# Token numbers in place of token rows in the slots of a grouped mixture of experts, and gathers in place of plain loads

## The chip, the core and the metric

The kernel runs on one core of a Trainium2 chip. The metric is the device time of one execution in microseconds. An execution taken with the hardware profiler gives the views that are read here; its times are in microseconds from the start of the span, unless said otherwise. The engines are TensorE (PE, with its weight loads PEld), VectorE (DVE), ScalarE (ACT), GpSimd (POOL) and SyncE (SP, which here only issues transfers).

## The reference, cut to what matters

The program is a chain of four blocks on x, 1250 tokens of 512 numbers, each with a residual: a message-passing layer over 40,000 edges, a grouped mixture of experts, a two-layer graph attention network, and an expert-choice mixture. The change concerns the second:

```python
z = layernorm(x, ln_g, ln_b)
gw = topk_gate(x @ wg_group, 2, G)                  # G = 4 groups
for g in range(G):
    iw = topk_gate(z @ wg_inner[g], 2, E)           # E = 8 experts in a group
    moe = sum(iw[:, e] * (relu(z @ W1[g, e] + b1[g, e]) @ W2[g, e] + b2[g, e]) for e in range(E))
    out += gw[:, g] * layernorm(z + moe, gln_g[g], gln_b[g])
```

As only two of four groups count for a token, and two of eight experts in each, a token needs four of the 32 experts: 5000 pairs of token and expert.

## The kernel before, in words

Everything is float32. 1250 tokens are ten chunks of 125 (`P`), a chunk's tokens on the partitions. The stages follow one another in one program, and a scheduler that knows the tiles places the waits; each engine runs its instructions in the order in which they were built.

**The edge stage** (0 to some 740 us) sorts the edges and runs 45 beats over them. In each beat a function `side(s)` does something besides: it stores two blocks of 128 rows of zeros (256 KB each) to `zs_d`, 88 in all, on SP's queue (L1996), until all of `zs_d` holds zeros; and it makes small products for the attention later. The sums of the edges go to the DRAM tile `sums_d`.

**The experts' slots.** In DRAM `zs_d` has 32 times `SL` = 208 rows, one stretch of slots for each expert, and behind these the rows of tiles of 128 for what does not fit in an expert's 208. Before the change a slot holds a token's row of 512 numbers, then the expert's output for it, in the same place.

**`grouped_moe`** does this in order:

1. For each of five blocks (`blk`) of two chunks: load the sums (`acc`, SP, L77), transpose them on TensorE (`transpose`, L95), project, add to x, normalise. VectorE and then POOL (L1008, one addition for each chunk) make the rows `z`. ScalarE and TensorE make the logits (`nT` L998, `lg` L1003), `top2` picks groups and experts.
2. Still in the block: a product with a triangular matrix on TensorE (L1027) counts how many earlier tokens chose the same expert, and so gives each pair its place in the slots; VectorE makes the four slots of each token (`slots`, `p4i`, L1040). Then POOL issues eight indirect DMAs (two chunks, four pairs, L1043), each of which scatters 125 rows of `z`, 2 KB each, to `zs_d`. A pair beyond 208 has a slot out of bounds and is dropped.
3. In blocks 1 and 2 the call `adjacency` makes a part of the graph's adjacency for the attention: SP loads `adj`, TensorE transposes it (L95), ScalarE does two operations for each piece (`none` L829, `adjt` L830), POOL adds them (L831) and issues the stores to `adjT_d` (L77). Parts 0 and 1 are done here, parts 2 to 4 in the loop over experts (e = 1, 4, 7). After block 1 `load` issues the weights of experts 0 to 5 on SP (L879, L881).
4. After the blocks: the counts (L1056), where experts have more than 208 pairs (`more`, L1058, `te`, L1077), the place of every pair in `pair_slot` and, with the slots that fit sent out of bounds, in `over_slot`. Scores become weights, x takes its share (L1120).
5. The loop over 32 experts: `rows(e)` loads the expert's 208 rows as two halves of 104 (`zr`, SP, L1132), issued two experts ahead; TensorE transposes them (`pz`, L95) and does the first layer (`ph`, L1150), ScalarE the relu (`hT`, L1152), TensorE the second layer (`po`, L1159), VectorE adds the rows (`y`, L1161), and ScalarE's queue stores y to the same slots (L1162).
6. Under `tc.If(some > 0)` the tiles beyond: 40 scatters with `over_slot`, then a loop over the tiles that are used. With these inputs no expert has more than 208 pairs and this part is not run.
7. For each chunk POOL gathers the four outputs of each token by `pair_slot` (`ya`, L1215), VectorE and ScalarE normalise and weight them, and the attention stage begins.

What sets the order around the change: POOL runs scatters, additions of z, additions of adjt and the issue of adjT_d's stores in one line. SP runs the loads of weights, sums, adjacency and rows in one line. A DMA that must wait holds what is behind it on its queue.

The step that the change is about, and the load that reads it:

```python
st = nc.gpsimd.indirect_dma_start(
    out=zs_d, out_offset=bass.IndirectOffsetOnAxis(ap=p4i[:, i, j:j + 1], axis=0),
    in_=z[:, blk * BC + i, :], in_offset=None, bounds_check=GX * SL - 1, oob_is_err=False)
...
def rows(e):
    zr = sp.tile([HS, 2, D], F32, name="zr", bufs=4)
    nc.sync.dma_start(zr, zs_d[e * SL:(e + 1) * SL, :].rearrange("(j p) d -> p j d", p=HS))
```

Of the kernel before, what the change touches and what calls it, by code (L numbers as in the profile page):

```python
# [52 lines left out]
MOE_NT = max(4 * -(-(N - MOE_SL) // MOE_TS), (4 * N - 5 * (MOE_SL + 1 - MOE_TS)) // MOE_TS)  # L53
MOE_ROWS = 32 * MOE_SL + MOE_NT * MOE_TS
LN_EPS = 1e-5
# [779 lines left out]

def grouped_moe(k, x, sums_d, nb_d, adjT_d, finish, zs_d, W_out0, W_out1, ln_g, ln_b, wg_group, wg_inner,
                W1, b1, W2, b2, gln_g, gln_b):


# [7 lines left out]
    HC = H // 128  # L847
    SL, TS, NT = MOE_SL, MOE_TS, MOE_NT
    HS = SL // 2
# [4 lines left out]
    with ExitStack() as es:  # L854
        mp = es.enter_context(tc.tile_pool(name="moe", bufs=1, reuse_waits="tile"))
        pair_slot = mp.tile([P, NC, 4], I32, name="pair_slot")
        over_slot = mp.tile([P, NC, 4], I32, name="over_slot")
        iw = [[mp.tile([P, NC], F32, name=f"iw{a}{b}") for b in range(2)] for a in range(2)]
# [12 lines left out]
        teri = mp.tile([1, NT + 1], I32, name="teri")  # L871
        b1T = mp.tile([128, GX * HC], F32, name="b1T")
        sw = ExitStack()
# [10 lines left out]
        with ExitStack() as s1:  # L884
# [86 lines left out]
            for blk in range(NB):  # L971
# [69 lines left out]
                for i in range(BC):  # L1041
                    for j in range(4):
                        st = nc.gpsimd.indirect_dma_start(  # L1043
                            out=zs_d, out_offset=bass.IndirectOffsetOnAxis(ap=p4i[:, i, j:j + 1], axis=0),
                            in_=z[:, blk * BC + i, :], in_offset=None, bounds_check=GX * SL - 1,
                            oob_is_err=False)
# [76 lines left out]
        with ExitStack() as s2:  # L1123
# [43 lines left out]
            for e in range(GX):  # L1167
# [5 lines left out]
                if e + 2 < GX:  # L1173
                    zr.append(rows(e + 2))
                zT = expert(zT, w1, w2, b1T[:, e * HC:(e + 1) * HC], 2, HS,
                            lambda: turned(zr.pop(0), 2, HS) if zr else None,
                            zs_d[e * SL:(e + 1) * SL, :])

            some = nc.values_load(teri[0:1, NT:NT + 1], min_val=0, max_val=NT,
                                  skip_runtime_bounds_check_because="a count of tiles")  # L1180
            with tc.If(some > 0):
                for c in range(NC):
                    for j in range(4):
                        st = nc.gpsimd.indirect_dma_start(
                            out=zs_d, out_offset=bass.IndirectOffsetOnAxis(ap=over_slot[:, c, j:j + 1],
                                                                          axis=0),
                            in_=z[:, c, :], in_offset=None, bounds_check=MOE_ROWS - 1, oob_is_err=False)
                        tc.declare_no_dep(st.ins, group="beyond", reason="slots of different pairs")
                        tc.add_to_no_dep_group("beyond", st.ins)
                for i in range(NT):  # L1190
# [7 lines left out]
                    nc.sync.dma_start(b, b1f[bass.ds(e, 1)].rearrange("o (k p) -> p (o k)", p=128))  # L1198
                    r0 = GX * SL + i * TS
                    z1 = sp.tile([TS, 1, D], F32, name="z1")  # L1200
# [744 lines left out]
def kernel(  # L1945
# [13 lines left out]
    xup_d = dram.tile([N, SW], F32, name="xup_d")  # L1959
    sums_d = dram.tile([CARRY + 256, SUMS], F32, name="sums_d")  # L1960
    nb_d = dram.tile([NC, P, N], BF16, name="nb_d")
# [3 lines left out]
    r_d = dram.tile([NC * 8, P], F32, name="r_d")  # L1965
    zs_d = dram.tile([MOE_ROWS, D], F32, name="zs_d")
    n_d = dram.tile([N, D], F32, name="n_d")
# [5 lines left out]
    with ExitStack() as turned:  # L1973
        with tc.tile_pool(name="xres", bufs=1, reuse_waits="tile") as xp:
# [13 lines left out]
            with tc.tile_pool(name="keep", bufs=1, reuse_waits="tile") as keep:  # L1988
# [14 lines left out]
            def finish():  # L2003
# [5 lines left out]

            grouped_moe(k, x, sums_d, nb_d, adjT_d, finish, zs_d, W_out0, W_out1, ln_g, ln_b, wg_group, wg_inner, fW1, fb1, fW2, fb2,  # L2010
                        gln_g, gln_b)
# [32 lines left out]
```

## Time and profile before

| | |
|---|---|
| time, median of ten runs | 2285.82 us (2278.57 to 2298.63) |
| profiled execution, its own time | 2285.86 us |
| its span | 2284.1 us, granted TensorE clock 0.915 |
| HBM read, written | 326.25 MB, 133.33 MB |
| `zs_d<-zero` stores | 88 of 256 KB, started between 112 and 684 us |
| `zs_d<-z` scatters | 40, median 1192 ns, started between 828.0 and 925.0 us |
| `zr<-zs_d` loads | 32 of 416 KB, started between 932.9 and 1151.0 us |
| `ya` gathers | 40, median 1211 ns, started between 1185.9 and 1260.2 us |

In the profile a group of instructions is named by line, engine, operation and the tiles out<-in, with the partitions and the elements of each. In a timeline a row gives the start, the busy time, and in brackets how long the engine was idle before and what released it. Neighbouring instructions of one kind are taken together, with their number behind an x. A helper such as the transpose of L95 gives one line to many calls, which are told apart by their tiles. A row of DMA_INDIRECT is the time that POOL spends on issuing it; the transfer lands later.

### The profile page before, as it was taken

How to read it: one execution, taken by the hardware profiler on the slowest of the kernel's cores; microseconds unless marked ns; L12 is line 12 of the kernel's file. 1: busy time of each engine (PE TensorE's matmuls, PEld its weight loads, DVE VectorE, ACT ScalarE, POOL GpSimd, SP SyncE). 2: the span in 40 equal slices, each digit the busy share in tenths (PEclk: the TensorE clock that was granted, in tenths of full speed). 3: DMA queues.
4: the chain of work that ended last, by engine and by line, in shares of the span. 5: the costliest groups of instructions: out<-in, count | busy, mean ns of one | idle time of the engine just before them, and what ended most of it. 6: DMA issues, size and time to landing. Idle time of an engine off the chain costs nothing. (4 is left out here: it accounts for less than half of the span.)

```text
span 2284.1 us, 31188 instructions
## 1 busy us (share of the span) xinstructions
PE 1954.7 (86%) x10813; PEld 1116.4 (49%) x10813; DVE 1387.1 (61%) x2944; ACT 1019.7 (45%) x1856; POOL 794.7 (35%) x671
## 2 busy tenths in 40 slices
PE   2499999999999564699988978999999999808997
PEld 2233333333333264466643337886447777605664
DVE  8188998988788167233327479874917667392000
ACT  2167777777777234221115427783306555101221
POOL 3367777777777055310027200000000000102342
PEclk9699999999999766799986889999999999858999
DMA  6779999899898496899835342304302221275752
GB/s 174 219 254 315 312 328 309 301 314 310 294 299 289 133 277 169 232 291 287 270 96 152 94 131 57 91 19 106 95 14 69 68 67 50 84 258 178 218 126 35
DMA packets 196586, 421.75 MB, mean 185 GB/s; under 512 B 66411, under 2 KB 86090, under 8 KB 192818
## 3 DMA queue, kind: packets, MB, share of 16 engines
q0 software_dynamic: 60416, 204.33, 28.4%
q1 hardware_dynamic: 116400, 183.36, 26.3%
q10 hardware_dynamic: 19599, 31.92, 4.4%
q8 instruction: 90, 1.47, 0.3%
q14 instruction: 81, 0.66, 0.1%
HBM read 326.25 MB, written 133.33 MB: 201 GB/s over the span
## 5 line engine op out<-in xcount | busy, mean ns | idle before, releaser
L528 POOL DMA_INDIRECT s<-xup_d,idx x360 | 439.1, 1220 | 163.5 <-issue 80.8
L597 DVE TENSOR_TENSOR m<-w,s 128x768 f32<-128x768 f32 x360 | 328.7, 954 | 92.0 <-ACT w L588 45.6
L1553 PE MATMUL po<-h,p 125*125 125x257 f32 x1600 | 363.9, 385 | 20.3 <-ACT p L1546 20.3
L1553 PEld LDWEIGHTS po<-h,p 125*125 125x125 f32 x1600 | 299.5, 190 | 71.8 <-ACT p L1546 23.1
L588 ACT COPY w<-pw 128x512 f32<-128x512 f32 x360 | 194.3, 593 | 106.7 <-PE pw L581 62.4
L1585 POOL TENSOR_TENSOR xc<-xc,fcb 125x512 f32<-125x512 f32 x10 | 18.1, 1822 | 609.5 <-DMA xc<-x_d 433.9
L581 PE MATMUL pw<-w,h 64*128 64x512 f32 x720 | 217.9, 651 | 6.1 <-issue 4.2
L1436 PE MATMUL ph<-w,xT 128*125 128x512 f32 x480 | 219.6, 616 | 1.9 <-ACT h L1441 0.7
L1532 ACT ACTIVATE q<-rr,ascol 125x250 f32<-125x250 f32 x400 | 166.0, 497 | 58.8 <-DVE p L1534 36.8
L1534 DVE SCALAR_TENSOR_TENSOR p<-rr,acol,q 125x250 f32<-125x250 f32 x400 | 171.9, 479 | 23.8 <-PE po L1553 14.7
L1436 PEld LDWEIGHTS ph<-w,xT 128*125 128x125 f32 x480 | 91.2, 194 | 123.9 <-issue 114.5
L620 PE MATMUL pa<-m,oh 128*32 128x256 f32 x2160 | 143.4, 383 | 0.1
L1488 DVE CUSTOM_DVE_ANT_0 junk<-row,nb 125x1250 bf16<-125x1250 f32 (+1 forms) x80 | 113.2, 1415 | 21.0 <-DMA row<-a_d 14.3
L600 DVE TENSOR_TENSOR m<-w,s 128x512 f32<-128x512 f32 x180 | 122.9, 683 | 0.0
L1538 DVE TENSOR_TENSOR p<-p,adjb 125x1250 f32<-125x1250 f32 x80 | 119.1, 1489 | 1.1
L1546 ACT ACTIVATE p<-p 125x1250 f32<-125x1250 f32 x80 | 98.0, 1240 | 46.6 <-DVE p L1538 34.9
L620 PEld LDWEIGHTS pa<-m,oh 128*32 128x32 f32 x2160 | 61.3, 109 | 117.0 <-issue 93.5
L1882 PE MATMUL po<-w,hT 128*78 128x512 f32 x256 | 116.3, 608 | 0.5 <-ACT hT L1874 0.5
L1159 PE MATMUL po<-w,hT 128*104 128x512 f32 x256 | 115.1, 592 | 0.0
L1161 DVE TENSOR_TENSOR y<-po,zr 104x512 f32<-104x512 f32 x64 | 44.3, 692 | 112.3 <-PE po L1159 110.0
L1827 DVE COPY xg<-px 128x624 f32<-128x624 f32 x16 | 12.9, 807 | 161.1 <-PE px L95 154.6
L1150 PE MATMUL ph<-zT,w 128*128 128x208 f32 x512 | 105.0, 349 | 6.3 <-ACT hT L1152 5.2
(461 smaller groups left out, 3030.6 us busy)
## 6 DMA issues: line engine op xcount, KB each, us to landing
w<-in_L_ffn_W SPq DMA_DIRECT2D x64, 512.0 KB
w<-in_L_ffn_w SPq DMA_DIRECT2D x32, 1024.0 KB
zs_d<-zero SPq DMA_DIRECT2D x88, 256.0 KB
zr<-zs_d SPq DMA_DIRECT2D x32, 416.0 KB
zs_d<-y ACTq DMA_DIRECT2D x32, 416.0 KB
adjb<-adjT_d SPq DMA_DIRECT2D x10, 1093.8 KB
rr<-r_d SPq DMA_DIRECT2D x8, 875.0 KB
attw<-in_L_gnn_W SPq DMA_DIRECT2D x12, 512.0 KB
```

The lines of the kernel that those rows point to most:

```text
L528: nc.gpsimd.indirect_dma_start(out=sj[:, u], out_offset=None, in_=xup_d, in_offset=bass.IndirectOffsetOnAxis(ap=idxs[s][:, i:i + 1], axis=0))
L581: nc.tensor.matmul(pw, nets[s][half, b * 128:(b + 1) * 128], w4[half, :], start=True, stop=True)
L588: nc.scalar.copy(made[s, t, jp][2][:, u].rearrange("p a d -> p (a d)"), made[s, t, jp][u])
L597: nc.vector.tensor_tensor(m[:, u, :, 1:4, :], w[:, u, 2:4, None, :].to_broadcast(shape), v[:, u, None, 1:4, :].to_broadcast(shape), op=ALU ...
L600: nc.vector.tensor_tensor(m[:, :, :, 0, :], w[:, :, 0:2, :], v[:, :, 0:1, :].to_broadcast([128, 2, 2, 128]), op=ALU.mult)
L620: nc.tensor.matmul(pab[q, 1, a::3 - a, :] if a < 2 else pab[q, 1, 2:4, :], oh[:, i, 1 + a, :], ms[j][:, 1, 0:2 + a:1 + a, :], start=first ...
L1436: self.k.nc.tensor.matmul(ph, self.xT[:, i, c * P:(c + 1) * P], self.w[half][i], start=i == 0, stop=i == kin - 1)
L1532: nc.scalar.activation(q[:, i], rr[:, hd, :, 1, :], AF.Identity, bias=ascol[:, c, hd:hd + 1])
L1534: nc.vector.scalar_tensor_tensor(p[:, i], rr[:, hd, :, 0, :], acol[:, c, hd:hd + 1], q[:, i], op0=ALU.add, op1=ALU.max)
L1538: nc.vector.tensor_tensor(pf, pf, adjb[:, half * HS:(half + 1) * HS, :] .rearrange("p c n -> p (c n)"), op=ALU.add)
L1553: nc.tensor.matmul(po[q], p[:, i, q, :], h[:, c, hd, :], start=c == 0, stop=c == NC - 1)
L1882: nc.tensor.matmul(py[:HCAP], hT[:, i, j * HCAP:(j + 1) * HCAP], w2[:, i, :], start=i == 0, stop=i == KH - 1)
```

## The change

The slots hold numbers, not rows. A new DRAM tile `tok_d` (64 times 104 float32: two halves for each expert) is first filled with numbers of tokens that exist (`whose`, an iota), so that a slot that nobody takes has a valid number. The 40 scatters write a token's number (`number`, 4 bytes) to its slots in `tok_d`. The rows `z` are stored once for each chunk to a new tile `z_d`, on SP's queue. After the last block SP reads `tok_d` back into `whose`, TensorE transposes it, VectorE turns it into integers (`token`, 104 on the partitions, 64 columns). `rows(e)` is now two indirect gathers on POOL, 104 rows each, from `z_d`.

`zs_d` is no longer written before the experts' outputs, so the zeros go. `zs_d` and `sums_d` become two views of one DRAM tile, with the slots behind the first `AT` rows, and the tiles beyond 208 lying where the sums were. `over_slot` goes; `pair_slot` now serves both uses, with other offsets.

```diff
+            number = tp.tile([P, NC], F32, name="number")
+            nc.gpsimd.iota(number, pattern=[[P, NC]], base=0, channel_multiplier=1,
+                           allow_small_or_imprecise_dtypes=True)
+            whose = tp.tile([2 * GX, HS], F32, name="whose")
+            nc.gpsimd.iota(whose, pattern=[[1, HS]], base=0, channel_multiplier=(N - HS) // (2 * GX),
+                           allow_small_or_imprecise_dtypes=True)
+            nc.sync.dma_start(tok_d, whose)
+            slot_d = tok_d.rearrange("e p -> (e p)")[:, None]
...
                     nc.gpsimd.tensor_tensor(z[:, c, :], z[:, c, :], lnb, op=ALU.add)
+                    spread(nc.sync, z_d[c * P:(c + 1) * P, :], z[:, c, :])
...
                         st = nc.gpsimd.indirect_dma_start(
-                            out=zs_d, out_offset=bass.IndirectOffsetOnAxis(ap=p4i[:, i, j:j + 1], axis=0),
-                            in_=z[:, blk * BC + i, :], in_offset=None, bounds_check=GX * SL - 1,
-                            oob_is_err=False)
+                            out=slot_d, out_offset=bass.IndirectOffsetOnAxis(ap=p4i[:, i, j:j + 1], axis=0),
+                            in_=number[:, blk * BC + i:blk * BC + i + 1], in_offset=None,
+                            bounds_check=GX * SL - 1, oob_is_err=False)
...
+            nc.sync.dma_start(whose, tok_d)
+            pt = ps.tile([HS, 2 * GX], F32, name="pl")
+            k.transpose(pt, whose)
+            nc.vector.tensor_copy(token, pt)
...
-            nc.vector.tensor_copy(pair_slot, p4)
             p4o = tp.tile([P, NC, 4], F32, name="p4o")
-            nc.vector.tensor_scalar(p4o, p4, float(GX * SL), FAR, op0=ALU.is_lt, op1=ALU.mult)
-            nc.vector.tensor_tensor(p4o, p4o, p4, op=ALU.add)
-            nc.vector.tensor_copy(over_slot, p4o)
+            nc.vector.tensor_scalar(p4o, p4, float(GX * SL), float(GX * SL + AT), op0=ALU.is_lt,
+                                    op1=ALU.mult)
+            nc.vector.scalar_tensor_tensor(p4o, p4, -float(GX * SL), p4o, op0=ALU.add, op1=ALU.add)
+            nc.vector.tensor_copy(pair_slot, p4o)
...
             def rows(e):
                 zr = sp.tile([HS, 2, D], F32, name="zr", bufs=4)
-                nc.sync.dma_start(zr, zs_d[e * SL:(e + 1) * SL, :].rearrange("(j p) d -> p j d", p=HS))
+                for j in range(2):
+                    nc.gpsimd.indirect_dma_start(
+                        out=zr[:, j, :], out_offset=None, in_=z_d,
+                        in_offset=bass.IndirectOffsetOnAxis(ap=token[:, 2 * e + j:2 * e + j + 1], axis=0))
                 return zr
...
                 def side(s):
-
-                    for b in range(2 * s, min(2 * s + 2, MOE_ROWS // 128)):
-                        nc.sync.dma_start(zs_d[b * 128:(b + 1) * 128, :], zero[:, :D])
                     if 4 <= s < 4 + len(steps):
                         steps[s - 4]()
```

More of the change, by code (lines that the diff above doesn't have):

```diff
@@ L53 @@
 MOE_NT = max(4 * -(-(N - MOE_SL) // MOE_TS), (4 * N - 5 * (MOE_SL + 1 - MOE_TS)) // MOE_TS)
-MOE_ROWS = 32 * MOE_SL + MOE_NT * MOE_TS
+MOE_AT = max(-(-(CARRY + 256) * SUMS // D), MOE_NT * MOE_TS)
+MOE_ROWS = MOE_AT + 32 * MOE_SL
 LN_EPS = 1e-5
@@ L832, in adjacency, with grouped_moe @@
     spread(nc.gpsimd, adjT_d[b], t.rearrange("p r i n -> p r (i n)"))
-def grouped_moe(k, x, sums_d, nb_d, adjT_d, finish, zs_d, W_out0, W_out1, ln_g, ln_b, wg_group, wg_inner,
+def grouped_moe(k, x, sums_d, nb_d, adjT_d, finish, z_d, tok_d, zs_d, W_out0, W_out1, ln_g, ln_b, wg_group, wg_inner,
                 W1, b1, W2, b2, gln_g, gln_b):
@@ L847, in grouped_moe @@
     HC = H // 128
-    SL, TS, NT = MOE_SL, MOE_TS, MOE_NT
+    SL, TS, NT, AT = MOE_SL, MOE_TS, MOE_NT, MOE_AT
     HS = SL // 2
@@ L856, in grouped_moe @@
         pair_slot = mp.tile([P, NC, 4], I32, name="pair_slot")
-        over_slot = mp.tile([P, NC, 4], I32, name="over_slot")
         iw = [[mp.tile([P, NC], F32, name=f"iw{a}{b}") for b in range(2)] for a in range(2)]
@@ L871, in grouped_moe @@
         teri = mp.tile([1, NT + 1], I32, name="teri")
+        token = mp.tile([HS, 2 * GX], I32, name="token")
         b1T = mp.tile([128, GX * HC], F32, name="b1T")
@@ L1176, in grouped_moe @@
                             lambda: turned(zr.pop(0), 2, HS) if zr else None,
-                            zs_d[e * SL:(e + 1) * SL, :])
+                            zs_d[AT + e * SL:AT + (e + 1) * SL, :])
             some = nc.values_load(teri[0:1, NT:NT + 1], min_val=0, max_val=NT,
@@ L1184, in grouped_moe @@
                         st = nc.gpsimd.indirect_dma_start(
-                            out=zs_d, out_offset=bass.IndirectOffsetOnAxis(ap=over_slot[:, c, j:j + 1],
+                            out=zs_d, out_offset=bass.IndirectOffsetOnAxis(ap=pair_slot[:, c, j:j + 1],
                                                                           axis=0),
-                            in_=z[:, c, :], in_offset=None, bounds_check=MOE_ROWS - 1, oob_is_err=False)
+                            in_=z[:, c, :], in_offset=None, bounds_check=NT * TS - 1, oob_is_err=False)
                         tc.declare_no_dep(st.ins, group="beyond", reason="slots of different pairs")
@@ L1198, in grouped_moe @@
                     nc.sync.dma_start(b, b1f[bass.ds(e, 1)].rearrange("o (k p) -> p (o k)", p=128))
-                    r0 = GX * SL + i * TS
+                    r0 = i * TS
                     z1 = sp.tile([TS, 1, D], F32, name="z1")
@@ L1959 @@
     xup_d = dram.tile([N, SW], F32, name="xup_d")
-    sums_d = dram.tile([CARRY + 256, SUMS], F32, name="sums_d")
+    long_d = dram.tile([MOE_ROWS * D], F32, name="long_d")
+    sums_d = long_d[:(CARRY + 256) * SUMS].rearrange("(r w) -> r w", w=SUMS)
+    zs_d = long_d.rearrange("(r w) -> r w", w=D)
     nb_d = dram.tile([NC, P, N], BF16, name="nb_d")
@@ L1965 @@
     r_d = dram.tile([NC * 8, P], F32, name="r_d")
-    zs_d = dram.tile([MOE_ROWS, D], F32, name="zs_d")
+    z_d = dram.tile([N, D], F32, name="z_d")
+    tok_d = dram.tile([64, MOE_SL // 2], F32, name="tok_d")
     n_d = dram.tile([N, D], F32, name="n_d")
@@ L2008, in finish @@
                 return k.gat, x1_d
-            grouped_moe(k, x, sums_d, nb_d, adjT_d, finish, zs_d, W_out0, W_out1, ln_g, ln_b, wg_group, wg_inner, fW1, fb1, fW2, fb2,
+            grouped_moe(k, x, sums_d, nb_d, adjT_d, finish, z_d, tok_d, zs_d, W_out0, W_out1, ln_g, ln_b, wg_group, wg_inner, fW1, fb1, fW2, fb2,
                         gln_g, gln_b)
```

## The prediction

> **What bounds the kernel now.** I read the page's shares, then busy time by stage, then the timelines of the one place where the order of stages puts several engines in a row. Page:
>
> ```profile
> PE 1954.7 (86%) x10813; PEld 1116.4 (49%) x10813; DVE 1387.1 (61%) x2944; ACT 1019.7 (45%) x1856; POOL 794.7 (35%) x671
> PE 33%; DVE 8%; ACT 2%; DMA 2%; issue 2%; POOL 1%; SPq 0%; POOLq 0%; ACTq 0%; DVEq 0%
> ```
>
> TensorE is busy 86% and carries most of the chain of work that ended last. The change adds one small product to TensorE, so it can only win or lose in its 329 us of idle time. By stage (columns: core, us, then busy us and instructions of PE, weight load, DVE, ACT, POOL, then clock, DMA share, GB/s):
>
> ```profile
> 520.00:680.00 160.00, 154.76 (x1312) 57.98 (x1315) 131.53 (x189) 115.39 (x180) 125.36 (x101) 1.00 0.90 298
> 690.00:740.00 50.00, 48.22 (x411) 17.84 (x415) 40.60 (x55) 36.16 (x57) 39.30 (x31) 1.00 0.84 282
> 860.00:865.00 5.00, 0.00 (x0) 0.00 (x0) 0.26 (x2) 0.60 (x1) 0.00 (x0) 0.50 0.33 123
> 980.00:1080.00 100.00, 95.42 (x442) 66.79 (x441) 31.91 (x40) 17.74 (x36) 7.32 (x7) 1.00 0.98 292
> ```
>
> The first two rows are the edge stage with and without the zeros (their last store starts at 684). The third lies in the routing of tokens, where TensorE stands still. The fourth is the loop over experts: TensorE 95%, DMA 98%. The end of the routing, by engine (start, us, engine, line, tiles, in brackets the idle time before it and its releaser):
>
> ```profile
> 902.01 1.27 POOL L1043 DMA_INDIRECT zs_d<-z,p4i  x1 [2.74 <-DVE t_r L1909]
> ...
> 924.97 1.19 POOL L1043 DMA_INDIRECT zs_d<-z,p4i  x1 [0.30 <-issue]
> 926.19 4.81 POOL L831 TENSOR_TENSOR adjt<-adjt,none 125x500 f32<-125x500 f32 x4
> ```
> ```profile
> 905.31 0.57 PE L1056 MATMUL pl<-run,ones 125*125 125x32 f32 x2
> 910.23 0.21 PE L95 MATMUL pl<-ident,te 36*1 36x36 f32 x1 [4.34 <-DVE te L1077]
> 910.37 1.20 PE L95 MATMUL pt<-ident,adj 125*125 125x125 f32 x4
> ...
> 937.83 1.62 PE L95 MATMUL pz<-ident,zr 104*128 104x104 f32 x8 [5.26 <-DMA zr<-zs_d]
> ```
>
> Sixteen scatters (blocks 3 and 4) leave POOL every 1.5 us (1.19 busy, 0.30 between) and end at E = 926.16. Under them TensorE does the counts (L1056), te and the transposes of the adjacency (L95). Then all wait for the last rows to land: SP issues zr at 932.87 (E+6.7), pz starts at 937.83 (E+11.7), and the first hT of ScalarE at 943.80 (E+17.6). This stretch and the stall at 860 are what the change can reach.
>
> **The change part by part.**
>
> *Zeros (88 stores of 256 KB, 112 to 684 us, L1996).* Without them the DMA share falls in the edge stage. TensorE's rate is the test: 1312 matmuls in 160 us is 8.20 per us with zeros, 411 in 50 us is 8.22 without. So the beat is not set by DMA, and the stores are hidden behind TensorE's own work; what their going could give is bounded by TensorE's idle time over 112 to 684, 16.7 us, and by the rates: 0.25% of 572 us is 1.4. I take 0, range -7 (some 40% of that idle) to 0.
>
> *Scatters (40, L1043).* The number stays; each now moves 125 times 4 bytes in place of 125 times 2 KB. POOL's time does not go by bytes: reading 125 rows takes 1.20 from zs_d at 2 KB and 0.98 to 1.97 from sums_d at 9 KB. I keep 1.2+0.3; nearest rows 0.95 and 1.6, on the 16 at the end -4 to +6. Landing is another matter. Now it is 6.7 us behind E (E to zr's issue). The small transfers of the trace that are awaited are aff_d<-at at 1.43 and affT<-aff_d at 1.71. I take 1.7, ends 1.43 and 6.6.
>
> [...] No row of before shows 4-byte writes by themselves. Were each as slow as a 2 KB row, landing would stay near 6.7 and the sum would be 5 higher.
>
> *z_d stores (10 chunks of two DMAs, SP).* By the order in which the built changed kernel's instructions stand, SP holds them ahead of the weights of experts 3 to 5 and of the accumulator loads of later blocks, and each waits for POOL's addition (L1008). The second half of block 2's sums is issued at some 833 in place of 817, lands near 842, and its transposes need it at 834: 8 late. But block 2 waited afterwards anyway, for ScalarE:
>
> ```profile
> 864.40 0.68 ACT L830 ACTIVATE adjt<-pt,tiny 125x500 f32<-125x500 f32 x1 [12.38 <-issue]
> ```
>
> That is ScalarE waiting 12.4 us for a buffer of adjt, whose store to adjT_d POOL issued at 854.51, behind sixteen scatters of 2 KB rows. With numbers in their place the queue is short and the store lands some 4 to 6 us sooner, so ScalarE goes on near 859. Late sums and early ScalarE meet: block 2 gets its products at 867 to 869, where it got them at 867.5. I take 0, ends -4 and +5.
>
> *POOL's addition of chunk 9.* It stood ahead of both groups of scatters (898.01); in the built order it stands between block 3's and block 4's. Its 1.27 us, off the path before, come into the row of scatters: **+1.3**, so E is 927.5.
>
> *The end of routing.* tok_d is read on SP behind the last scatter, transposed on TensorE (L95) and copied on VectorE into token. In the built order that transpose stands ahead of the counts, te and all adjacency transposes of this call, and the copy ahead of the VectorE chain that ends in pair_slot. What was done under the scatters, at 905 to 919, waits for the scatters' landing; and POOL has the first addition of adjt (L831) ahead of the first two gathers. From E:
>
> - landing 1.7, SP's issue 0.3, load of tok_d 1.7, transpose and copy 0.6 (0.21 and some 0.3): token at E+4.3;
> - counts 0.57, then the VectorE chain, te, transposes of adj, ScalarE's two operations, as they stood from 905.92 to 912.92, 7.0, of which about 0.8 was other work: 6.2; adjt at E+11.0;
> - POOL's addition 1.24: E+12.3;
> - two gathers of 104 rows at 1.08 (between 0.95 for 78 rows and 1.20 for 125) with 0.3 between, 2.5; landing 2.2, since in the later stage the second gather ended at 2058.43 and TensorE began on it at 2060.60: pz at E+17.0, against E+11.7.
>
> Then hT waits too. ScalarE is in order, and its fifth transposed piece (L829) needs a buffer that POOL's second addition frees; this stands behind six gathers: 12.3 + 6 times 1.38 + 1.24 = E+21.8, then 0.68 and 0.67 of ScalarE: hT at E+23.1, against E+17.6. The second product of expert 0 cannot start sooner. **+5.5**. This is the largest term and rests on order, not on a new duration. The copies and products among it fill TensorE's wait, so pz's own 5.3 is inside the 5.5. If a gather lands as a combine gather does (fourth of chunk 0 ended at 1191.83, VectorE began at 1196.06: 4.2), pz is at E+19, still under hT's wait.
>
> *Loop over experts.* 64 gathers at 1.38 are 88 us of POOL where it had 15 operations on adjt; 2.8 of 7.1 us per expert, hidden by TensorE's 95%. They are issued two experts ahead. Bytes are the same, 416 KB each. adjT_d's stores now stand among gathers, so the addition of a later block can be late by a gather or two: 0 to +3; I take 0. The y stores, combine and the part under the If are as before; pair_slot's extra operation is off the path.
>
> Sum: 0 + 0 + 1.3 + 5.5 + 0 = +6.8. On the profiled execution's 2285.9 (span 2284.1) that is 2292.7, rounded **2293**. The median of ten is 2285.82, so the base is the same.
>
> **Rivals.**
>
> *Relief of the queues decides (faster, about 2279).* For it: the DMA share is 0.98 in the loop and TensorE's idle there has a DMA's name; the stall at 860 is one of the queue. The sixteen scatters of 2 KB are 4 MB. If adjT_d lands by 858 and SP's late sums by 840, blocks 3 and 4 come 6.5 earlier (hT's stall of 12.4 cut in half), the scatters with them; the edge stage gives 3 and the loop's idle 4 more: -6.5-3-4+6.8 = -6.7, 2279. It decides if the last scatter starts before about 919. Against it: SP's order, which delays the same block, and the equal rates of the first two rows.
>
> *A wash (2287 to 2288).* Half of that, 4 to 5 us, comes without the edge's and the loop's share: 6.8-5 = +2.
>
> *Worse (about 2301).* SP held by the z_d stores delays block 2 by 5 (its sums land past 842), and later blocks' adjT_d is late by 3: 6.8+8 = +15. A 4-byte scatter that lands no sooner than a 2 KB one (+5, no relief of ScalarE, +3) gives the same.
>
> **How the numbers follow.** About 0.3%, 6.9 us, is what a measurement of this kernel can tell from no change: 2279 to 2292.7. Forecast 0.45 (2287 to 2299, a little over half above the bound); relief 0.17; wash 0.18; worse 0.20. Slower: 0.27 of the forecast and 0.20, 0.47. Same: 0.18 of each of forecast and wash, 0.36. Faster: 0.17. The range goes from the relief case, 2280, to the upper end of worse, 2303; below and above it I leave about 0.1 each.
>
> **What would show it.** In the changed kernel's profile: the edge stage at 8.2 matmuls per us (zeros hidden), or more (they were not); ScalarE's stall near 852 to 864 shorter and block 2's TensorE no earlier; the last scatter starting near 926 to 928; from its end to the first pz some 17 us, where it was 11.7, and to the first hT some 23, where it was 17.6; and between them the counts, te and transposes that were under the scatters. In the loop PE at 95% again, with POOL's gathers beside it. I am wrong if the transposes of adj start before the token transpose, if gathers go on POOL ahead of adjt's first addition, or if the scatters' pace is not 1.5 us.

## The result and the profile after

The changed kernel takes 2307.8 us (median of 13 runs, 2297.2 to 2313.0) where the kernel before takes 2285.5 (46 runs). The ratio is 1.0092, 95% interval 1.0078 to 1.0107: 18 to 24 us slower. The profiled execution has a span of 2302.9, 18.8 more than before. The forecast was slower by 7, with a range that ended at 2303: the sign was right, the size a third.

First the edge stage, by a stretch that the prediction shows for the kernel before (the columns are core time, busy us and instructions of PE, weight load, DVE, ACT, POOL, then clock, DMA share, GB/s):

```profile
520.00:680.00 160.00, 153.01 (x1304) 57.37 (x1307) 130.12 (x187) 114.88 (x178) 125.55 (x101) 1.00 0.82 259
```

The zeros are gone and the DMA share fell from 0.90 to 0.82, but TensorE's rate did not rise: 1304 matmuls in 160 us where it was 1312. The first transposes of the sums in block 0, the start of the routing, begin at 784.4 (784.0 before). So the loss lies behind that point. SP's waits between 780 and 945 (what it waited for: us in total, times, longest) and its timeline:

```profile
SPq L79 <- POOL z L1020: 68.5, 10, 20.6
```
```profile
819.37 3.68 SPq L79 DMA_DIRECT2D z_d<-z  x4
...
831.53 3.84 SPq L79 DMA_DIRECT2D z_d<-z  x4
...
840.40 2.46 SPq L79 DMA_DIRECT2D acc<-long_d  x4
...
872.22 2.64 SPq L79 DMA_DIRECT2D z_d<-z  x4
874.91 1.21 SPq L79 DMA_DIRECT2D acc<-long_d  x3
```

SP stands for 68.5 us with a store of z_d at its head that waits for POOL. Behind it are the loads of sums for blocks 2 to 4. Block 2's first load is issued at 840.4. In the kernel before it was issued at 813.9:

```profile
813.92 2.84 SPq L77 DMA_DIRECT2D acc<-sums_d  x4
```

TensorE stands for the sums. Its rows in the changed kernel, then in the kernel before (the rows of `sel,before` are block 2's product with the triangular matrix):

```profile
799.62 0.34 PE L97 MATMUL pl<-ident,b1r 64*128 64x64 f32 x1 [5.37 <-DMA b1r<-in_L_ffn_b]
...
854.23 1.90 PE L97 MATMUL pt<-ident,acc 125*128 125x125 f32 x8 [14.06 <-DMA acc<-long_d]
...
881.54 0.65 PE L1040 MATMUL pl<-sel,before 125*125 125x64 f32 x2 [7.76 <-DVE sel L1033]
```
```profile
834.11 1.88 PE L95 MATMUL pt<-ident,acc 125*128 125x125 f32 x8
...
867.52 0.52 PE L1027 MATMUL pl<-sel,before 125*125 125x64 f32 x2
```

Block 2's transposes begin at 854.2, where they began at 834.1, 20 us late; its product comes at 881.5 where it came at 867.5, 14 us late. So 6 us of the delay are made up between the two. A second delay is in this view, and the prediction had none of it: in block 0 TensorE waits 5.4 us for the constants b1r, where it had waited 1.0. ScalarE's wait for adjt's store, which was to cover late sums, is gone (0.5 us of idle time before L832, 12.4 before):

```profile
868.77 0.68 ACT L832 ACTIVATE adjt<-pt,tiny 125x500 f32<-125x500 f32 x1 [0.52 <-issue]
```

The end of the routing, on POOL and on TensorE:

```profile
924.08 1.26 POOL L1020 TENSOR_TENSOR z<-z,lnb 125x512 f32<-125x512 f32 x1
925.53 1.25 POOL L1056 DMA_INDIRECT tok_d<-number,p4i  x1 [0.19 <-issue]
...
936.07 1.19 POOL L1056 DMA_INDIRECT tok_d<-number,p4i  x1 [0.30 <-issue]
946.56 1.24 POOL L833 TENSOR_TENSOR adjt<-adjt,none 125x500 f32<-125x500 f32 x1 [9.31 <-ACT adjt L832]
947.99 1.02 POOL L1151 DMA_INDIRECT zr<-z_d,token  x1 [0.19 <-DVE t L979]
```
```profile
940.73 0.31 PE L97 MATMUL pl<-ident,whose 64*104 64x64 f32 x1 [20.86 <-DMA whose<-tok_d]
940.98 0.63 PE L1074 MATMUL pl<-run,ones 125*125 125x32 f32 x2
943.79 0.21 PE L97 MATMUL pl<-ident,te 36*1 36x36 f32 x1 [2.18 <-DVE te L1095]
943.93 1.20 PE L97 MATMUL pt<-ident,adj 125*125 125x125 f32 x4
...
952.60 1.96 PE L97 MATMUL pz<-ident,zr 104*128 104x104 f32 x8
```

The last scatter ends at E = 937.3 (926.2 before). This part went as foretold: the transpose of whose stands ahead, counts, te and adjacency follow, pz comes at E+15.3 and the first hT (958.91) at E+21.6; before they came at 11.7 and 17.6.

A table of the profiles, in us. The first column counts from the first transposes of the sums to the last scatter's end E, the second from E to the first hT, the third from there to the last hT of the loop, the fourth from there to the end of the span. Runs on other chips have a shorter edge stage (the kernel before takes 2249 to 2250 us there, and 2285 to 2287 where before, after, e1, e2, e3 and e8 ran), so only these columns and the ratios are compared. The kernel before has a profile from the slower kind alone. e2_z_at_end and e2_again are one kernel on two chips: single profiles of it differ by 1.1 us in the routing, 2.0 in the loop and 3.7 in the rest.

| kernel | routing to E | E to hT | loop | rest | ratio of times, 95% interval |
|---|---|---|---|---|---|
| before | 142.1 | 17.6 | 231.4 | 1108.9 | 1 |
| after | 152.8 | 21.6 | 234.7 | 1109.3 | 1.0092 (1.0078 to 1.0107) |
| e2_z_at_end | 140.8 | 21.3 | 234.7 | 1109.2 | 1.0019 (1.0003 to 1.0034) |
| e2_again | 139.7 | 21.7 | 232.7 | 1105.5 | 1.0018 (1.0003 to 1.0033) |
| e5_before_z_store | 156.8 | 16.3 | 234.1 | 1113.9 | 1.0065 (1.0042 to 1.0088) |
| e1_z_on_pool | 151.8 | 21.4 | 232.0 | 1106.2 | 1.0088 (1.0059 to 1.0116) |
| e3_token_late | 154.4 | 15.2 | 243.9 | 1109.6 | 1.0120 (1.0099 to 1.0141) |
| e8_z_end_token_late | 139.1 | 14.8 | 244.0 | 1113.2 | 1.0032 (1.0013 to 1.0050) |
| e9_adjacency_ahead | 147.3 | 20.1 | 234.4 | 1112.1 | 1.0026 (1.0009 to 1.0043) |
| e10_init_on_pool | 144.2 | 21.7 | 237.3 | 1105.9 | 1.0047 (1.0031 to 1.0064) |
| e11_b1r_first | 134.1 | 21.5 | 232.9 | 1110.0 | 0.9993 (0.9979 to 1.0007) |
| e13_after_b1r_first | 148.9 | 21.1 | 233.2 | 1107.9 | 1.0069 (1.0049 to 1.0089) |
| e12_adjacency_before_scatter | 137.7 | 21.2 | 231.5 | 1111.5 | 0.9980 (0.9963 to 0.9998) |
| e6_zeros_back | 140.3 | 21.5 | 237.7 | 1110.7 | 1.0027 (1.0011 to 1.0043) |
| e7_plain_rows | 139.6 | 21.0 | 235.8 | 1107.1 | 1.0036 (1.0024 to 1.0048) |

From before to after: 10.7 in the routing, 4.0 behind E, 3.3 in the loop, 0.8 elsewhere.

### The profile page after: what moved, and what is told of

It reads as the page before. It is cut to its first block, busy times and chain, and to the rows that moved or that the text cites. A ratio compares the mean times of both kernels' runs of the same rounds, so it can differ in the third digit from the quotient of the medians.

```text
span 2302.9 us, 31197 instructions
## 1 busy us (share of the span) xinstructions
PE 1953.9 (85%) x10814; PEld 1115.6 (48%) x10814; DVE 1394.0 (61%) x2944; ACT 1020.2 (44%) x1856; POOL 857.0 (37%) x737
## 5 line engine op out<-in xcount | busy, mean ns | idle before, releaser
L1567 ACT ACTIVATE p<-p 125x1250 f32<-125x1250 f32 x80 | 98.0, 1241 | 50.1 <-DVE p L1559 41.5
L1151 POOL DMA_INDIRECT zr<-z_d,token x64 | 63.5, 992 | 127.1 <-DVE y L1182 116.1
```

## The experiments

The theory after the result: SP is held by the stores of z_d (some 11 us of the routing), and the order behind the last scatter costs 4. The rivals: late constants in block 0, or the scatters themselves.

### The stores of z_d behind the blocks (e2_z_at_end, e2_again)

```diff
-                    spread(nc.sync, z_d[c * P:(c + 1) * P, :], z[:, c, :])
...
+            for c in range(NC):
+                spread(nc.sync, z_d[c * P:(c + 1) * P, :], z[:, c, :])
             nc.sync.dma_start(whose, tok_d)
```

> The changed kernel with the ten stores of z_d on SP written behind the five blocks. They then stand on SP behind all loads of sums. Theory (SP is held): block 2's first transposes begin at 834 to 840, the last scatter at 925 to 928, and the time falls by 8 to 11 us, to 2297 to 2300; what is left over the kernel before is the order behind the last scatter, 4 us, and the loop, 3. Rival (late constants of block 0, POOL's added addition between the scatters, or the 4-byte scatters): the last scatter at 932 or later and no more than 4 us gained.

The ratio went from 1.0092 to 1.0019, some 17 us, more than expected. SP's timeline, in an execution that reached block 0 some 10 us later than the changed kernel's:

```profile
834.10 1.74 SPq L79 DMA_DIRECT2D acc<-long_d  x4
...
840.88 23.84 SPq L79 DMA_DIRECT2D acc<-long_d  x8
864.83 12.54 SPq L79 DMA_DIRECT2D z_d<-z  x12
```

All loads of sums are out before the first store waits, and E comes 140.8 after the first transposes, 12.0 sooner than in the changed kernel. A second series on another chip gave the same:

> The kernel of e2_z_at_end once more, beside the two others on one chip. The ratio to the kernel before was 1.0019, interval 1.0003 to 1.0034; the same is expected, 1.000 to 1.004.

1.0018, E at 139.7. The hold on SP is the main cause.

### The stores alone, in the kernel before (e5_before_z_store)

```diff
                     nc.gpsimd.tensor_tensor(z[:, c, :], z[:, c, :], lnb, op=ALU.add)
+                    spread(nc.sync, z_d[c * P:(c + 1) * P, :], z[:, c, :])
```

> The kernel before with one addition: the rows z are also stored to z_d on SP's queue, each chunk behind POOL's addition, as the changed kernel does; nobody reads them. Theory (SP is held): the loads of sums behind these stores come late as in the changed kernel, block 2's first transposes at 848 to 855 in place of 834, the last scatter at 933 to 938 in place of 925, and the time rises by 8 to 14 us over the kernel before, to 2294 to 2301. Rival, the step of the prediction (the late sums are covered by ScalarE's wait for the store of adjT_d): within 4 us of the kernel before.

1.0065, about 15 us, and E comes 14.7 later in the profile. SP waits as in the changed kernel, and TensorE stands 18 us for the second half of block 2's sums:

```profile
SPq L77 <- POOL z L1008: 74.2, 7, 20.1
```
```profile
818.77 1.90 PE L95 MATMUL pt<-ident,acc 125*128 125x125 f32 x8 [17.97 <-DMA acc<-sums_d]
```

The expectation was wrong on which half comes late: the first half's transposes begin 50.3 us after the first ones (50.1 before), the second half's at 73.8 (55.6 before). The stores of ten chunks that nobody reads cost some 0.7 of what the whole change costs. The rival, the prediction's own step, falls.

### The stores on POOL's queue (e1_z_on_pool)

```diff
-                    spread(nc.sync, z_d[c * P:(c + 1) * P, :], z[:, c, :])
+                    spread(nc.gpsimd, z_d[c * P:(c + 1) * P, :], z[:, c, :])
```

> The changed kernel with the stores of z_d issued on POOL's queue, each behind the addition that makes the rows, in place of SP's. Theory (SP is held): in the changed kernel SP waited 68.5 us for POOL's additions ahead of the loads of sums, so that block 2's first transposes began at 854.2 where they had begun at 834.1 and the last scatter at 936.1 where it had been 925.0. Without that hold the transposes of block 2 begin at 834 to 840. POOL has twenty more issues of some 0.6 us, so the last scatter begins at 926 to 931: 5 to 10 us faster than the changed kernel, 2298 to 2303. Rival (block 0's constants, which landed 5 us later, and the scatters themselves made the delay): the last scatter stays at 934 or later, the time at 2306 or more.

No gain that the times show (1.0088), and E at 151.8. SP is free: block 2's transposes begin 59.0 after the first ones (69.8 in the changed kernel, 50.1 before). But POOL now issues both halves of adjT_d's store behind sixteen scatters, and ScalarE waits for it:

```profile
871.32 0.68 ACT L832 ACTIVATE adjt<-pt,tiny 125x500 f32<-125x500 f32 x1 [15.28 <-DMA adjT_d<-adjt]
```

The hold moved from one queue to another. That the theory gave this kernel 5 to 10 us was wrong: it counted issues, and not who stands behind them.

### The steps of token behind pair_slot (e3_token_late, e8_z_end_token_late)

```diff
-            nc.sync.dma_start(whose, tok_d)
-            pt = ps.tile([HS, 2 * GX], F32, name="pl")
-            k.transpose(pt, whose)
-            nc.vector.tensor_copy(token, pt)
...
             nc.vector.tensor_copy(pair_slot, p4o)
+            nc.sync.dma_start(whose, tok_d)
+            pt = ps.tile([HS, 2 * GX], F32, name="pl")
+            k.transpose(pt, whose)
+            nc.vector.tensor_copy(token, pt)
```

> The changed kernel with the load, transpose and copy that make token written behind pair_slot, so that the counts, te and the VectorE chain stand ahead of them. SP's stores of z_d stay where they are. Theory (order behind the last scatter costs 4 us): the last scatter stays near 936; from its end to the first hT it takes 16 to 18 us where the changed kernel took 21.7, and the time falls by 3 to 5, to 2303 to 2305. Rival (the chain of landing, load, transpose, gather and landing sets it, whatever stands around it): 21 us again, the time within 2 us of 2308.

e8 has the edit of e2 as well:

> Both edits: the stores of z_d behind all loads of sums, and the steps of token behind pair_slot. If the two causes are separate and are what the theory says, their gains add: 8 to 11 and 3 to 5, so 2292 to 2297, and the loop's 3 us and some of the routing are left over the kernel before. If the first cover (ScalarE's wait for adjT_d's store, 12.4 us in the kernel before) is gone too, as the short scatters let that store land sooner, block 2 comes up to 6 us earlier and the time is 2286 to 2291. If one of the two is no cause, 2298 or more.

The order does what was said of it: from E to hT 15.2 and 14.8 us, better than before's 17.6. The time does not follow: 1.0120, and 1.0032 beside e2's 1.0019. The loop takes 9 us more and gives all back, in e3 more than all. The first 40 us of it, in the changed kernel and in e8:

```profile
958.00:998.00 40.00, 38.72 (x183) 27.91 (x182) 12.43 (x17) 13.17 (x23) 21.06 (x22) 0.97 0.99 296
```
```profile
939.00:979.00 40.00, 32.44 (x141) 22.39 (x140) 9.34 (x13) 10.91 (x18) 15.82 (x16) 0.91 0.82 244
```

ScalarE's longest waits in these 40 us of e8:

```profile
ACT nb L822 <- DVE adj L820: 11.2, 2, 5.9
```

In the changed kernel all 20 transposes of part 2 of the adjacency stand ahead of the first expert's products. In e8 eight of them run among the experts' products, the last at 947.8, and the next part's load goes out only then, at 948.5. ScalarE waits 11.2 us for that part, and TensorE 4.6 us for the hT that stands behind it on ScalarE. That this order is the cause rests on these rows and on e9, where moving part 2 brought the loop back. e8's 2293 (by its ratio) lies in the band of the sum, but by two changes of opposite sign and not by the gains adding up.

### Part 2 of the adjacency ahead of token (e9_adjacency_ahead)

```diff
-            nc.sync.dma_start(tok_d, whose)
+            nc.gpsimd.dma_start(tok_d, whose)
...
+            adjacency(k, ap, ps, 3, sums_d, nb_d, adjT_d, 2)
             nc.sync.dma_start(whose, tok_d)
...
-                if e in (1, 4, 7):
+                if e in (4, 7):
```

> e8_z_end_token_late with the first store of tok_d on POOL, and the call that makes part 2 of the adjacency moved from the loop over experts to a place ahead of token. In e8 the steps of token stood ahead of this part's loads and transposes, so that ScalarE met them within the first two experts and TensorE idled 13 us more there. Theory: the first hT comes 16 to 18 us after the last scatter's end, as in e8, and the loop takes 231 to 236 us as in the kernel before and not 244: with block 0's 5 us 2280 to 2286, no slower than the kernel before. Rival (the loop is set by the DMA engines, so that what starts earlier waits later): hT early, the loop 240 or more, 2288 to 2294.

The loop is back at 234.4, as expected. The rest is a miss: E to hT is 20.1, since POOL's additions and stores for the moved part stand ahead of the first gathers, and E itself comes at 147.3 (e9 has the edit of e10 as well, where E comes at 144.2). 1.0026, no better than e2. No place for this work was found that costs nothing.

### The first store of tok_d on POOL (e10_init_on_pool)

On e2:

```diff
-            nc.sync.dma_start(tok_d, whose)
+            nc.gpsimd.dma_start(tok_d, whose)
```

> e2_z_at_end with the first store of tok_d (valid numbers for slots that nobody takes) on POOL's queue in place of SP's. In the changed kernel it stood on SP between the first two loads of sums and waited 2.8 us for POOL; the loads of block 0 came 3 us later, the adjacency's load overtook the constants b1r, and TensorE waited 5.3 us for these. Theory: block 0's triangular product begins some 30 us after the first output projection, as before, where it was 34 to 37; then the scatters, the store of adjT_d and ScalarE's wait come 5 us earlier too, as that store now lands 4 to 5 us after its issue where it took 9.9: the time falls by 3 to 6 us, to 2286 to 2289. Rival (that wait is covered by another in block 2): block 0 earlier, the last scatter and the time unchanged, 2290 to 2293.

It fell. TensorE's wait for b1r stays (the view of its waits):

```profile
PE pl L97 <- DMA b1r<-in_L_ffn_b: 4.8, 1, 4.8
```

SP's first load of adj was issued at 751.23 here, b1r at 751.75. In the changed kernel they came at 791.35 and 791.29, in the kernel before adj at 792.43 and b1r at 790.81, and in e5, which has the short wait too, at 753.09 and 751.84. So in these four kernels b1r is late where the first load of adj (1.2 MB in four DMAs) goes out with it (waits of 4.8 and 5.4 us), and not where adj goes out 1.2 us and more behind it (1.5 in e5, 1.0 in the kernel before). That adj is the cause was not tested by itself, and what in the change shifts this by a microsecond was not settled. E came later as well, 144.2 where e2 had 140.8 and 139.7: TensorE waits 14.3 us for VectorE's selection (10.6 in e2_again), and e12 shows a reason for such a wait.

### b1r first (e11_b1r_first, e13_after_b1r_first)

```diff
+            b1r = tp.tile([GX * HC, 128], F32, name="b1r")
+            nc.scalar.dma_start(b1r, b1f.rearrange("x (k p) -> (x k) p", p=128))
             lng = tp.tile([P, D], F32, name="lng")
...
             spread(nc.scalar, lnb, bcast_rows(ln_b, P))
-            b1r = tp.tile([GX * HC, 128], F32, name="b1r")
-            nc.scalar.dma_start(b1r, b1f.rearrange("x (k p) -> (x k) p", p=128))
```

On e2:

> e2_z_at_end with the load of the constants b1r issued ahead of those of lng and lnb. In all kernels with the change so far TensorE waits 4 to 5 us in block 0 for b1r, where the kernel before waited 1.0: there SP's first load of adj (1.1 MB) was issued 1.6 us behind b1r, here together with it or ahead of it. Theory: with b1r first, TensorE no longer waits for it, block 0's triangular product begins some 30 us after the first output projection as in the kernel before (34 to 37 in the changed ones), the last scatter ends 127 to 130 us after it (132.4 in e2, 134.2 before), and the time falls by 3 to 5 us, to between 1.0 to 0.9985 of the kernel before. Rival: other waits of block 2 take its place, the last scatter ends at 131 or later after it, the ratio stays at 1.0015 to 1.003.

0.9993 beside e2_again's 1.0018 on the same chip: 5.6 us, and the change costs nothing any more. E comes at 134.1, 5.6 sooner than in e2_again. (The expectation counts from the first output projection, which this edit moves; the table counts from the first transposes.) On the changed kernel itself:

> The changed kernel with the load of b1r ahead of those of lng and lnb, and SP's stores of z_d where the change put them. Theory (late b1r is a second cause, in series with SP's hold, since SP waits for additions of z that come later by as much): block 0's triangular product some 29 us after the first output projection in place of 35.5, the last scatter's end at 137 to 140 after it in place of 144.7, the time 5 to 7 us under the changed kernel's, ratio 1.006 to 1.007. Rival (SP's hold covers it): 144 again and a ratio of 1.0085 to 1.0105.

1.0069, as expected, with E at 148.9 where it was 152.8. The late constants are a second cause of 4 to 6 us, which adds to the hold on SP and is not covered by it.

### adjT_d's store sooner (e12_adjacency_before_scatter)

On e11, the call of `adjacency` for blocks 1 and 2 is written ahead of the block's scatters:

```diff
+                if blk in (1, 2):
+                    adjacency(k, ap, ps, 3, sums_d, nb_d, adjT_d, blk - 1)
                 for i in range(BC):
                     for j in range(4):
                         st = nc.gpsimd.indirect_dma_start(
...
-                if blk in (1, 2):
-                    adjacency(k, ap, ps, 3, sums_d, nb_d, adjT_d, blk - 1)
```

> e11_b1r_first with the call that makes a part of the adjacency written ahead of the block's scatters. POOL then issues the second half of adjT_d's store behind eight scatters and not sixteen, 12 us earlier, so that ScalarE's wait for it in block 2 (9.7 us in e11, 12.4 before) goes. Theory: that wait sets block 2; without it the last scatter ends 5 to 10 us sooner after the first output projection than e11's 124.7, and the time falls below both kernels, ratio 0.995 to 0.998. Rival: block 2's sums or VectorE are late next, less than 3 us gained, ratio 0.998 to 1.0.

ScalarE's wait is gone (0.33 us of idle time, 9.72 in e11), and block 2 is not sooner: its product comes 82.2 us after the first transposes, 78.0 in e11. ScalarE, then TensorE's waits between 745 and 890:

```profile
811.12 0.68 ACT L832 ACTIVATE adjt<-pt,tiny 125x500 f32<-125x500 f32 x1 [0.33 <-issue]
```
```profile
PE pl L1039 <- DVE sel L1032: 22.4, 3, 11.2
```

TensorE waits for VectorE's selection in place of ScalarE, 22.4 us where the same view of e11 has 11.2, and E is at 137.7, 3.6 later than there. The selection is late by one operation. On VectorE, and on POOL at the same time:

```profile
814.79 9.46 DVE L1928 TENSOR_TENSOR t_h<-lg,t_m 125x80 f32<-125x80 f32 x1
```
```profile
815.69 2.49 POOL L1020 TENSOR_TENSOR z<-z,lnb 125x512 f32<-125x512 f32 x2
818.13 6.01 POOL L833 TENSOR_TENSOR adjt<-adjt,none 125x500 f32<-125x500 f32 x5
```

The same operation takes 0.24 us in the changed kernel's last block (at 914.76), with no addition of POOL beside it. Here it takes 9.46 and ends 0.1 us after POOL's seven additions. ScalarE's early end let POOL do its additions of adjt in a row with those of z, under the selection; in e11 the five of adjt begin at 819.42, when the selection is done. So e12 does not show what block 2 would do with neither wait: its edit put another in place of ScalarE's. That POOL's additions hold VectorE rests on these rows and not on an experiment. The ratio, 0.9980, is the lowest of all and just under 1, but e11's interval overlaps it and the profile has no gain over e11 in the routing, so it is not shown that this edit helps.

### The zeros, and plain loads (e6_zeros_back, e7_plain_rows)

e6 is e2 with the zeros stored to a tile of their own:

```diff
                 def side(s):
+                    for b in range(2 * s, min(2 * s + 2, 88)):
+                        nc.sync.dma_start(spare_d[b * 128:(b + 1) * 128, :], zero[:, :D])
                     if 4 <= s < 4 + len(steps):
```

> The kernel of e2_z_at_end with the 88 stores of zeros put back into the edge stage, to a tile that nobody reads. The prediction put the zeros at 0 (0 to 7 us). If they were hidden the time is within 2 us of e2_z_at_end's 2291.5 and the edge stage ends within 1 us; if they cost, it is 3 to 7 us longer, and the edge stage with it.

1.0027 beside 1.0019 and 1.0018, not told apart. In the edge stage, 112 to 650 us, TensorE is busy throughout with the zeros (e6) and without (e10, on the same chip):

```profile
112.00:650.00 538.00, 538.00 (x4593) 201.82 (x4583) 487.10 (x824) 408.43 (x626) 430.37 (x350) 1.00 0.94 323
```
```profile
112.00:650.00 538.00, 538.00 (x4585) 201.82 (x4583) 487.11 (x825) 408.77 (x625) 430.41 (x350) 1.00 0.88 284
```

On this chip the zeros were hidden. Where the kernel before takes 2285 to 2287 us, TensorE has idle time in this stage (16.7 us from 112 to 684 in the kernel before), and the routing began at 784.0 with the zeros (the kernel before) and between 781.2 and 794.2 without them (five profiles), so that a gain of a few us is neither seen nor excluded there.

e7 is e2 with the two gathers replaced; it leaves out the choice of rows:

```diff
-                for j in range(2):
-                    nc.gpsimd.indirect_dma_start(
-                        out=zr[:, j, :], out_offset=None, in_=z_d,
-                        in_offset=bass.IndirectOffsetOnAxis(ap=token[:, 2 * e + j:2 * e + j + 1], axis=0))
+                lo = (e * SL) % (N - SL)
+                nc.sync.dma_start(zr, z_d[lo:lo + SL, :].rearrange("(j p) d -> p j d", p=HS))
```

> e2_z_at_end with each expert's rows loaded by one plain load on SP from z_d, as many rows as before but not the expert's own, in place of POOL's two gathers; token is still made, and nobody reads it. It leaves out the choice of rows. Theory (the gathers cost by what they wait for behind the last scatter, and nothing in the loop): the first hT comes at least 4 us sooner after the last scatter's end than e2's 21.3, the loop is 231 to 238 us as in all kernels, and the time is 3 to 6 us under e2's, ratio 0.999 to 1.001. Rival (64 gathers of 2.8 us per expert cost in the loop): the loop is 3 us or more under every other kernel's, 228 or less.

Half of the theory fell: without these gathers E to hT is 21.0, as with them, and the ratio is 1.0036 where 0.999 to 1.001 was expected. So the 4 us behind E are not the gathers' issue and landing but the place of whose's transpose ahead of counts, te and adjacency, which e3 and e8 changed and e7 did not. In the loop, 235.8 without the gathers and 232.7 to 234.7 with them, they cost nothing.

## Why the prediction was wrong

- **The step that failed is the one on the z_d stores**, "I take 0, ends -4 and +5". It named the queue, the lines behind it and the wait. Its sizes were wrong. It gave a delay to the second half of block 2's sums alone, issued at 833, there at 842, 8 us late. In the run both halves stood behind the stores: the first load went out at 840.4, and TensorE had the sums at 854.2, 20 us later than before. Some 5 us of this come from the late b1r of block 0 (with b1r first, e13, block 2's first load goes out 50.5 us after the first transposes, in the changed kernel 56.0). In e5, where b1r is on time, the second half's transposes are still 18 us late. Four weight loads stood between the stores and the sums, and in block 2 the stores at 872.2 held three more loads of sums. e2 and e5 price the step at 15 to 17 us of time, 12 to 15 of profile.
- **The cover took up a part.** The step set its 8 us against ScalarE's wait of 12.4. Between block 2's transposes and its product, 20 us of delay became 14. Something else was late there as well: in the changed kernel VectorE's selection for block 2 runs under POOL's additions (870.93 to 880.07), and six of its operations that take 0.16 to 0.24 us in its last block (914.76 to 917.30), where POOL only issues scatters, take 0.89 to 1.26, which adds up to some 5 us. An idle time with a name is slack only up to what is late next.
- **A term was missing**: b1r, 4 to 6 us (e11, e13). Nothing in the diff touches it.
- **Relief of the queue came**, as the step and the rival of the queues had it: from the issue of adjT_d's second half to ScalarE's next instruction 9.9 us before, 3.9 in e2 and 4.6 in e8. With both delays away (e11) the routing is 8.0 shorter than before, and that pays for the 3.9 behind E. How much of the 8.0 is this relief was not tested by itself; block 2's product comes 5.5 sooner.
- **The routing's 10.7 us add up** from the profiles: 12.0 for the hold (the changed kernel less e2), 5.6 for b1r (e2_again less e11), -8.0 (e11 less the kernel before), and the 1.1 by which the two profiles of e2's kernel differ.
- **The rival "worse"** had the hold on SP as its cause and came nearest, 2301. It too counted 5 us for the hold, where 12 were measured, and nothing for b1r, so that its number was near partly by luck.
- **4-byte scatters**: pace 1.5 us, as taken (1.19 busy and 0.30 between, with 4 bytes as with 2 KB). Landing 1.4 (E to SP's issue of whose at 938.66; taken 1.7; before 6.7). Under the last sixteen scatters POOL's queue took 58.3% of the DMA engines' time before and 7.1% after. The small ones took less of the engines' time here and landed sooner than the rows that they replaced. The 0.98 to 1.97 us that the prediction took for a read of sums_d belong to a scatter into it (sums_d<-out,sum_rows), which is the nearer row.
- **POOL's addition of chunk 9**, +1.3: there, but chunk 9's slots (p4i) were ready at 922.6 and the addition fills 924.1 to 925.3, so at most this much is on the path.
- **The end of routing**, +5.5: measured +4.0 (pz at E+15.3 for 17.0, hT at 21.6 for 23.1), by the order that was read. That this order, changed, would give the 4 us back was not forecast and is not so: the loop takes them.
- **Zeros**, 0: right on e6's chip; where the edge stage is longer it is not settled. **Loop**, 0: 3.3 in the profile, 3.0 of it in products at a lower granted clock (below); without the gathers (e7) the loop takes 235.8.

## What to carry to other kernels

Stores that waited for a computed value held all that stood behind them on SP's queue here (68.5 us of waits in the changed kernel): before adding such a transfer, list the loads behind it that feed an earlier stage, and put it behind them (here one moved loop was worth 17 us). When a delay is set against a stall that is there already, ask what that stall's end waits for and what is late next. Delays that lie in one chain add, as those of b1r and of SP's queue did here. And a stage's times may only be read from the old timeline as long as nothing ahead of it has moved.

## What the runs showed of the hardware

TensorE has a pause of some 3 us for hT in the loop of at least eight of the profiles (2.78 to 3.55: before, after, e2_again, e6, e10 to e13). The changed kernel, from 1038 us on by 2 us:

```profile
1038.00:1040.00 2.00, 0.47 (x1) 0.47 (x2) 0.00 (x0) 0.43 (x1) 0.00 (x0) 0.66 1.05 314
1040.00:1042.00 2.00, 2.00 (x7) 1.94 (x7) 0.00 (x0) 0.00 (x0) 0.00 (x0) 0.50 1.09 284
1042.00:1044.00 2.00, 2.00 (x4) 1.00 (x4) 0.00 (x0) 0.43 (x1) 0.00 (x0) 0.50 1.05 252
1044.00:1046.00 2.00, 2.00 (x4) 0.77 (x3) 0.11 (x1) 0.00 (x0) 0.00 (x0) 0.63 1.04 391
```

After a pause of 3.02 us the granted clock is halved for some 6.8 us (0.34 + 0.5 + 0.5 + 0.37 of 2 us each, over one half). The eight products of ph behind the pause take 3.14 us and the eight of po 5.10. In the kernel before the same pause, 3.04 us, left the clock at 1.00, and they take 1.67 and 3.60: a difference of 3.0 us, about the loop's 3.3. e5, whose rows are loaded plainly, has such slow products too (the longest of po in its loop takes 1061 ns, as in the changed kernel, the median 592). Of one kernel's two profiles e2 has them (1061 ns) and e2_again, with a pause of 3.55, has none over 595. So the loop's 3.3 us belong to the profiled execution; that the change brings the drop about is not shown. Nor is what decides over it: the products of ph behind the pause take 2.01 to 3.14 us after pauses of 2.78 (e10), 2.83 (e13), 2.99 (e11) and 3.42 us (e6), and 1.67 after 3.00 (e12) and 3.55 (e2_again).

VectorE's selection was drawn out while POOL added: one operation of 125x80 took 9.46 us in e12 under seven additions of POOL; in the changed kernel it took 1.26 in block 2 under such additions (at 872.92) and 0.24 in the last block without them (at 914.76).

The same kernel takes 2287 us on one chip and 2249 to 2250 on others, 1.7% apart, more than anything studied here; only ratios within a chip can be compared.
